# Summing a selective scan over its states chunk by chunk instead of half chunk by half chunk, in a Mamba plus mixture-of-experts block

## The chip, the cores and the metric

The kernel runs on one core of a Trainium2 chip. The metric is the device time of one execution in microseconds (us), as a median over executions. A core has five instruction queues that matter here: PE (the matrix engine; PEld are its weight loads), DVE (vector), ACT (scalar functions), POOL (a second vector engine) and SP (which only issues DMAs). Each queue runs its instructions in the order in which they were written and stops at the first one whose inputs are not ready.

## What is computed

The input is x of shape 4 x 512 x 256 in float32. First a Mamba layer with its norms and its residual, then a mixture of experts with the same:

```
proj = LN(x) @ in_proj.T;  xs, gate = split(proj)              # 512 channels each
xt   = silu(causal depthwise conv of 4 taps(xs) + conv_b)
ts, B, C = split(xt @ x_proj.T)                                # 16, 16, 16
dt   = softplus(ts @ dt_proj.T + b)
state[d,s] = state[d,s] * exp(dt[d] * A[d,s]) + dt[d] * B[s] * xt[d]     # over the time t
y[d] = sum over s of state[d,s] * C[s]                         # 16 states
x    = x + LN((y + xt * D) * silu(gate) @ out_proj.T)
out  = x + LN(shared expert / 5 + 4/5 * top-4 of 16 experts(LN(x)))
```

## The kernel before

**Tiling.** The 2048 tokens are cut into 8 units n of 256 tokens (two units are one sequence). The 512 channels are cut into 4 chunks c of 128. A chunk's states are laid on the partitions as 32 channels x 4 states, so a chunk needs 4 state groups g times 2 pairs p, which makes 8 slots; a unit has 32 slots and the kernel 256. In a slot k, ACT writes exp(dt A) into a PSUM tile `h` (L493, two instructions of 128x256), DVE runs the recurrence over 128x512 in place (`scan`, L777), and DVE multiplies with C into `hc` (`times_c`, L785), of which a ring of 11 buffers exists. POOL makes dt B x for two slots at a time (`dbx`, L505). `rep` (dt and dt x repeated over the partitions) and `bt`, `ct` (B and C likewise) come back through DRAM.

**The sum over the states.** `sum_y` (L791) adds the 4 states on neighbouring partitions, and the 4 state groups, by matmuls with the constant `sel` (128x32): each takes 32 output columns of the array and writes 32 partitions of the PSUM tile `y`, of which there is one bank. It is called for YS = 4 slots at a time, so twice per chunk and 64 times in all. One call is 8 matmuls; a float32 matmul stands in the profile as two instructions, so a call is 16 of them. When a chunk's second call is done, `close` (L811, DVE) adds D xt, `gated_y` (L817, POOL) multiplies with the gate, and `out_proj` (L887, PE) projects two chunks at a time. A chain of small steps (norm, add, norm, transpose, router, top 4) follows, and then the 10 pairs of experts of that unit: `h1`, `h3` (L1041, PE), tanh and a copy (ACT), `gated` (L1060, DVE), `weighted` and `product` (L1056 and L1063, POOL), `down` (L1072, PE). Ahead of the scans a unit needs its `front`: norm, `in_proj` (L391), `conv` (L406, PE), `x_proj` (L434), `dt_proj` (L457), softplus, and stores.

**The head.** `first()` (L509) writes unit 0's front by hand. Its end is: `x_proj`, with four spare matmuls between its halves (`warm`, L310: a 128x128 product whose result nobody reads); `ssm` on ACT; `dt_proj`; `softplus` on ACT (L463); then four groups of matmuls with `rsel` (L560) which repeat dt and dt x over the partitions for chunk 0; their copies on DVE (L563); the first exps and the first dbx. 

**Who sets the order.** Everything else is a task of the class `Plan`. A task has an engine, a duration booked by hand, a due rank (mostly its slot number), what it depends on and which ring buffers it takes. `Plan.order` (L179) plays the tasks forward with those durations and picks, on the engine that could start soonest, the task of the lowest rank among those that could start within a patience. The tables SHIFTS and PATIENCE move ranks and patience per kind of task and unit. The result is one fixed order per engine. In it, the loop at the end of the kernel fills gaps that the plan leaves on PE before the first `down` with spare matmuls, one for each 0.22 us.

Of the kernel before, what the change touches and what calls it, by code (L numbers as in the profile page):

```python
# [24 lines left out]
CI = DI // P  # L25
# [10 lines left out]
CP = CG // NJ  # L36
CSL = SG * CP
SLOTS = CI * CSL
YS = 2 * CP
FR = 42  # L40
START = 16
CH = HS // H
# [12 lines left out]


SHIFTS = dict(
    fA=(0, -12.75, 3, -15.25, 45, 15.25, 6.5, -4),
    fB=(-1.25, -13, -10, 37.25, 25.25, 41.5, 0, -11.5),
    fC=(-54, -5.25, 6, -12.75, -37.75, 17.5, -35, 24.75),  # L60
    fD=(-12, 19.5, -4, -8.5, -1.25, 44.5, -41.5, -33.5),
    exps=(14.5, 48.75, 33.5, 0, -49, 5.25, -9, 0),
    dbx=(15.25, -9.75, 10, 6, 4.75, 40.75, -9.5, 15.75),
    scan=(54.75, 16.75, -3.75, 59, 8.5, -7.75, -20, -1.5),
    hc=(37.75, -41.25, 48.5, -15.75, 3.75, 52.25, 5.75, -8.5),
    keep=(57, 0, 0.25, 0, 0, 0, 18.75, 0),
    sum=(-5, -7, 28, 41, -11.5, 11.25, 25.5, -3.5),
    close=(2.5, 19.5, 17, 12.25, 10.25, -33.5, -53, 24.5),
    ld=(0, -0.75, -11.75, 1.5, -8, -21.5, 0.75, 1.5),
    bc=(0.25, 0, 11, -13.25, 0.75, -5.75, -49, 2.75),  # L70
    chain=(-5.25, -30.5, -52, -53, -33, -45, -0.25, 6),
    load=(-20.25, -23.5, -56.75, -22.25, 2, -38.25, 0, -5.5),
    h1=(51.75, 9.5, -2.75, 11.25, 24, 23.5, 7.5, 28.75),
    h3=(28.5, -0.25, -56.5, -51.25, 2.5, 3, 4.25, 10.75),
    act=(7, 44.5, -2.25, 0, -10.25, 28.5, 10.75, 0),
    gated=(-8, -9, -29.25, -2.25, -60, -54.75, -31, -10),
    prod=(36.5, 3, -6, 5, -41, -46.25, 15.75, 23.5),
    down=(-8.5, 40.5, -32, 9.5, -10.25, 14, -8, 29.5),
    fin=(11.75, 1.25, -15, 8.5, -5.75, 29, 2.25, -6.5),
)  # L80

PATIENCE = dict(
    fA=(1.5, 1, 0.3, 0.1, 0.6, 0.6, 0.3, 0.6),
    fB=(1, 0.1, 0.1, 0.1, 0.6, 0.1, 0.1, 0.1),
    fC=(1, 0.1, 0.6, 1, 0.6, 0.1, 0.1, 0.1),
    fD=(0.6, 0.3, 0.1, 0.1, 0.1, 0.3, 0.1, 0.6),
    exps=(0.1, 0.3, 0.1, 0.1, 0.6, 0.1, 0.1, 0.1),
    dbx=(2.2, 0.3, 0.1, 0.1, 0.3, 1.5, 0.6, 0.1),
    scan=(0.1, 0.1, 0.1, 0.1, 2.2, 0.3, 0.1, 0.6),
    hc=(0.1, 0.1, 0.6, 0.3, 1.5, 2.2, 0.1, 0.1),  # L90
    keep=(0.1, 0.1, 0.1, 0.1, 0.3, 0.1, 2.2, 0.1),
    sum=(0.3, 0.6, 0.3, 0.6, 0.1, 0.3, 0.6, 0.1),
    close=(0.1, 0.1, 1.5, 0.1, 0.3, 0.3, 0.6, 1.5),
    ld=(1, 0.3, 0.1, 1.5, 0.1, 0.1, 0.1, 0.1),
    bc=(0.3, 1, 1.5, 0.6, 1, 2.2, 0.1, 0.1),
    chain=(0.6, 0.1, 0.1, 0.1, 0.1, 0.1, 0.1, 0.6),
    load=(0.6, 1, 0.3, 2.2, 1.5, 2.2, 1.5, 0.6),
    h1=(0.1, 0.3, 0.1, 0.3, 1.5, 1, 0.1, 2.2),
    h3=(0.1, 0.6, 0.1, 0.3, 1, 0.1, 0.3, 0.3),
    act=(0.6, 0.1, 0.3, 0.6, 0.3, 1, 0.1, 2.2),  # L100
    gated=(0.3, 0.6, 0.1, 0.3, 0.1, 0.3, 0.1, 1.5),
    prod=(0.6, 0.1, 0.3, 0.1, 0.1, 0.1, 0.6, 1),
    down=(0.1, 2.2, 0.1, 1.5, 0.1, 0.1, 0.1, 2.2),
    fin=(0.1, 0.1, 0.3, 0.1, 0.3, 0.1, 0.6, 2.2),
)

GROUPS = dict(
# [6 lines left out]
    scan=(SLOTS, "scan"),  # L114
    hc=(SLOTS, "hc"),
    keep=(SLOTS, "keep"),
    sum=(SLOTS // YS, "sum"),
    close=(CI, "close yg"),
    ld=(CI, "reps loadxg decay0 decay1 delta"),
    bc=(1, "bc"),  # L120
# [127 lines left out]
def mamba_then_moe(ctx: ExitStack, tc: tile.TileContext, a: dict, out: bass.AP):  # L248
# [61 lines left out]
    def warm(n, bank):  # L310
        t = ps.tile([P, P], F32, name=bank)
        for _ in range(n):
            T.matmul(t, ident, ident, start=True, stop=True)  # L313
# [111 lines left out]
                ALU.add, ALU.mult,  # L425
            )

    def x_proj(n, bank, between=lambda: None):

        t = q["x", n] = ps.tile([P, U // 2], F32, name=bank)  # L430
        q["ssm", n] = ring(work, [P, U // 2], "ssm")
        for c in range(CI):
            for h in range(2):
                T.matmul(  # L434
                    t[ts(h, P // 2), :], w_x[:, c, :], q["xt", n, c // 2][:, c % 2, ts(h, U // 2)],
                    start=c == 0, stop=c == CI - 1,
                )
            if c == 1:
                between()

    def ssm(n):
        S.activation(q["ssm", n], q["x", n], AF.Identity, bias=one_row)
# [66 lines left out]
    def first():  # L509
        st = stats_of(xs[0])  # L510
        rstd = stat.tile([P, NU], F32, name="rstd")
        G.tensor_scalar(rstd, st[:, :, 2], 1.0 / D, EPS, ALU.mult, ALU.add)
        G.tensor_tensor(rstd, rstd, mhalf, ALU.pow)
        xn = ring(work, [P, NU, D], "xn")
        for i in range(NU):
            V.tensor_scalar(
                xn[:, i, :], xs[0][:, i, :], st[:, i, 1:2], rstd[:, i : i + 1],
                ALU.subtract, ALU.mult,
            )
        xn_t = q["xn_t", 0] = ring(work, [P, CD, U], "xn_t")  # L520
        for k, nm in enumerate(("f", "h1")):
            t = ps.tile([P, U], F32, name=nm)
            for i in range(NU):
                T.transpose(t[:, ts(i, P)], xn[:, i, ts(k, P)], ident)
            (V.tensor_copy if k else S.copy)(xn_t[:, k, :], t)
        make_taps()
        for m in range(2):
            in_proj(0, m, ("h3", "y")[m])
        for m in range(2):
            xp = q["pad", 0, m] = ring(work, [P, 2, KC - 1 + U], "xp")  # L530
            G.memset(xp[:, :, 0 : KC - 1], 0.0)
            copy = V.tensor_copy if m else S.copy
# [12 lines left out]
        store_bc(0)  # L545
        rp = reps[0] = ring(work, [P, CG, 2, U], "rep")
        us = [ring(work, [P, 2, U], "u") for m in range(2)]
        dt_proj(0, ("po", "h1"))
        softplus(0)
        dt = [q["sp", 0][:, ts(m, 2), :] for m in range(2)]  # L550
        load_bc(0)
        G.tensor_tensor(us[0][:, 0, :], dt[0][:, 0, :], q["xt", 0, 0][:, 0, :], ALU.mult)

        banks = iter("f h3 y po".split())
        spread = {}
        for h in range(2):
            for w, src in enumerate((dt[0][:, 0, :], us[0][:, 0, :])):
                t = spread[h, w] = ps.tile([P, 2, U], F32, name=next(banks))
                for j in range(2):
                    T.matmul(t[:, j, :], rsel[:, 2 * h + j, :], src, start=True, stop=True)  # L560
        for h in range(2):
            for w in range(2):
                V.tensor_copy(rp[:, ts(h, 2), w, :], spread[h, w])  # L563
        for i in range(2):
            exps(i)
        inputs_of(0, 2)
        G.tensor_tensor(us[0][:, 1, :], dt[0][:, 1, :], q["xt", 0, 0][:, 1, :], ALU.mult)
        for w, t in enumerate((dt, us)):
# [250 lines left out]
    for k in range(N * SLOTS):  # L819
# [32 lines left out]
        if n % UB == 0:  # L852
            add(("keep", k), "ACT", 0.06, k - 1, lambda k=k: keep(k),
                [("scan", k)] + ([("delta", i - CI)] if n else []), (), [("h", k)])
        if k % YS == YS - 1:
            s = k // YS
            fresh = k % CSL == YS - 1
            last = c == CI - 1 and not fresh
            add(("sum", s), "PE", 1.0, k - 3 if last else k + 2, lambda k=k: sum_y(k - YS + 1),
                [("hc", k)] + ([("sum", s - 1)] if s else []),  # L860
                [("y", ("y", i))] if fresh else [], [("hc", j) for j in range(k - YS + 1, k + 1)] + [("y", i)])
            if not fresh:
                add(("close", i), "DVE", 0.385, k - 3 if last else k + 3, lambda n=n, c=c: close(n, c),
                    [("sum", s), ("loadxg", i)], (), [("y", i), ("xgt", i)])
                add(("yg", i), "POOL", 0.685, k - 3 if last else k + 3, lambda n=n, c=c: gated_y(n, c),
# [5 lines left out]
    def chain(n):  # L871
# [115 lines left out]
        def store_cw():  # L987
# [270 lines left out]
```

## Time and profile before

| | |
|---|---|
| median of 3 runs (lowest, highest) | 701.21 us (701.19, 704.19) |
| the profiled execution: its own time, its span | 703.04 us, 701.2 us |
| mean granted clock of the matrix engine | 0.993 of full speed |
| scan L777 | 256 instructions, 1220 ns each |
| hc L785 | 256 instructions, 680 ns each |
| dbx L505 | 129 instructions, 2346 ns each |
| expert matmuls L1041 and L1072 | 1280 and 640 instructions, 296.4 and 152.5 us busy |
| sum matmuls L799 | 1024 instructions, 385 ns each, 68.7 us busy |
| spare matmuls L313 | 212 instructions, 28.5 us busy |

The span runs from the first to the last instruction of the execution; the execution's own time has 1.84 us more around it. Busy time is the union of an engine's instructions, so matmuls that overlap on the array are counted once: 1024 of 385 ns make 68.7 us. The chain of waits goes back from the last instruction, at each step to what released it. The windows view gives each engine's busy time in a stretch, the number of its instructions in brackets, and the clock that was granted to the matrix engine.

### The profile page before, as it was taken

The numbers are of one execution on the slowest core, as the hardware profiler recorded it, in microseconds if no ns is written. First come the engines' busy times: TensorE is split into PE (matmuls) and PEld (weight loads), VectorE is DVE, ScalarE is ACT, GpSimd is POOL, SyncE is SP. The second block draws the span as 40 slices with busy tenths as digits, with TensorE's granted clock in tenths as the row PEclk, the third lists the DMA queues.
The fourth block names the chain that finished last, engine by engine and source line by source line (L and its number), as shares of the span: only waits on it lengthen the run. The fifth ranks groups of instructions, "written<-read, shape, count | busy, mean of one in ns | idle before, by whom it ended". The sixth has DMA issues, their size and how long they took to land.

```text
span 701.2 us, 13359 instructions
## 1 busy us (share of the span) xinstructions
PE 678.9 (97%) x4468; PEld 540.3 (77%) x4468; DVE 575.2 (82%) x814; ACT 492.9 (70%) x1308; POOL 603.6 (86%) x607
## 2 busy tenths in 40 slices
PE   8899998999999998999999999999999999999996
PEld 7777676767777776888777787778877787888885
DVE  3598999899999998998999979979899879942111
ACT  2599979889777868686888876877787767723220
POOL 1498569999999999999999999999999999975644
PEclk9999999999999999999999999999999999999999
DMA  5298766586847886669668687779687754563650
GB/s 165 101 323 275 241 209 211 161 287 220 300 164 223 278 267 208 202 241 306 235 201 269 220 263 232 243 232 318 208 254 243 243 193 151 181 212 127 218 209 18
DMA packets 84697, 155.16 MB, mean 221 GB/s; under 512 B 9842, under 2 KB 33266, under 8 KB 84628
## 3 DMA queue, kind: packets, MB, share of 16 engines
q1 hardware_dynamic: 83796, 152.99, 65.9%
q10 hardware_dynamic: 832, 1.31, 0.5%
q8 instruction: 35, 0.57, 0.3%
q14 instruction: 34, 0.28, 0.1%
HBM read 135.27 MB, written 19.01 MB: 220 GB/s over the span
## 4 chain that ended last, share of the span: by engine, by line
PE 59%; DVE 15%; ACT 11%; POOL 11%; issue 3%; POOLq 0%; DVEq 0%; ACTq 0%
PE h L1041 29%; PE po L1072 14%; DVE h L777 8%; ACT h L493 5%; PE y L799 5%; DVE hc L785 4%; POOL dbx L505 4%; PE f L894 3%; POOL g L1063 2%; PE f L391 2%; POOL g L1056 2%; PE f L406 1%; PE f L313 1%; ACT xn L355 1%; DVE q L1060 1%
## 5 line engine op out<-in xcount | busy, mean ns | idle before, releaser
L777 DVE TENSOR_TENSOR_SCAN h<-h,dbx 128x512 f32<-128x512 f32 x256 | 308.2, 1220 | 21.4 <-POOL dbx L507 8.8
L505 POOL TENSOR_TENSOR dbx<-rep,bt 128x1024 f32<-128x1024 f32 (+1 forms) x129 | 302.1, 2346 | 21.2 <-DVE h L777 16.4
L1041 PE MATMUL h<-xn_t,w 128*128 128x256 f32 x1280 | 296.4, 383 | 1.3 <-ACT g L1053 1.0
L493 ACT ACTIVATE h<-rep,a_rep 128x256 f32<-128x256 f32 x512 | 244.8, 478 | 57.2 <-DVE hc L785 43.9
L1041 PEld LDWEIGHTS h<-xn_t,w 128*128 128x128 f32 x1280 | 240.9, 191 | 43.5 <-issue 4.4
L785 DVE TENSOR_TENSOR hc<-h,ct 128x512 f32<-128x512 f32 x256 | 170.3, 680 | 3.9 <-ACT carry L789 1.8
L1072 PE MATMUL po<-w,g 128*128 128x256 f32 x640 | 152.5, 383 | 0.9 <-POOL g L1063 0.9
L1072 PEld LDWEIGHTS po<-w,g 128*128 128x128 f32 x640 | 119.1, 190 | 24.7 <-issue 4.5
L1063 POOL TENSOR_TENSOR g<-g,q 128x512 f32<-128x512 f32 x80 | 101.7, 1272 | 10.5 <-DVE q L1060 7.7
L1060 DVE SCALAR_TENSOR_TENSOR q<-th,h 128x512 f32<-128x512 f32 x80 | 54.5, 681 | 55.6 <-PE h L1041 54.4
L1056 POOL TENSOR_TENSOR g<-g,cwb 128x512 f32<-128x512 f32 x64 | 81.6, 1274 | 16.9 <-ACT g L1053 16.5
L1048 ACT ACTIVATE th<-h 128x512 f32<-128x512 f32 x80 | 47.6, 595 | 57.8 <-PE h L1041 57.5
L799 PE MATMUL y<-hc,sel 128*32 128x256 f32 x1024 | 68.7, 385 | 0.1
L799 PEld LDWEIGHTS y<-hc,sel 128*32 128x32 f32 x1024 | 27.4, 109 | 29.8 <-issue 14.7
L496 ACT COPY h<-zero 128x1 f32<-128x1 f32 x256 | 41.7, 163 | 8.2
L391 PE MATMUL f<-xn_t,w_in 128*128 128x256 f32 x176 | 42.6, 385 | 1.5 <-DVE gate L739 1.2
L391 PEld LDWEIGHTS f<-xn_t,w_in 128*128 128x128 f32 x176 | 32.6, 190 | 9.2 <-DVE gate L739 1.3
L1053 ACT COPY g<-h 128x512 f32<-128x512 f32 x64 | 37.2, 581 | 0.0
L789 ACT COPY carry<-h 128x2 f32<-128x2 f32 x128 | 19.3, 159 | 22.8 <-DVE h L777 14.7
L406 PE MATMUL h<-xp,taps 64*64 64x256 f32 x288 | 29.5, 381 | 0.6 <-DVE xt L423 0.6
L894 PE MATMUL f<-w_out,yg 128*128 128x256 f32 x112 | 26.6, 382 | 0.0
L406 PE MATMUL f<-xp,taps 64*64 64x256 f32 x208 | 25.3, 382 | 0.9 <-POOL delta L771 0.6
(163 smaller groups left out, 607.5 us busy)
## 6 DMA issues: line engine op xcount, KB each, us to landing
w<-in_w SPq DMA_DIRECT2D x80, 512.0 KB, 5.1
rep<-rep SPq DMA_DIRECT2D x124, 256.0 KB, 4.3
w<-in_w SPq DMA_DIRECT2D x80, 256.0 KB, 4.4
cwb<-cwd SPq DMA_DIRECT2D x64, 256.0 KB, 4.8
xg<-xg SPq DMA_DIRECT2D x32, 256.0 KB, 4.6
bt<-bc SPq DMA_DIRECT2D x8, 512.0 KB, 6.2
ct<-bc SPq DMA_DIRECT2D x8, 512.0 KB, 6.9
xg<-gate SPq DMA_DIRECT2D x16, 256.0 KB, 5.8
```

What stands on the lines that cost most here:

```text
L391: T.matmul(t[:, j, :], w_in[:, k, ts(2 * m + j, P)], q["xn_t", n][:, k, :], start=k == 0, stop=k == CD - 1,)
L406: T.matmul(t[j][half[r ^ j], :], taps[half[r], 2 * m + j, k, :], q["pad", n, m][half[r], j, k : k + U], start=k == 0, stop=k == KC - 1,)
L493: S.activation(h[:, j, :], dt[:, m, 0, :], AF.Exp, scale=a_rep[:, c, g, m : m + 1])
L505: G.tensor_tensor(t[:, m], reps[n * CI + c][:, m, 1, :], bt[:, m], ALU.mult)
L777: V.tensor_tensor_scan(flat, flat, dbx[:, ts(p, NJ), :].rearrange("p j t -> p (j t)"), 0.0, ALU.mult, ALU.add)
L785: V.tensor_tensor(hc, expo[k], ct, ALU.mult)
L799: T.matmul(ys[n, c][m * CS : (m + 1) * CS, :], sel, hcs[k][:, j, :], start=g == 0, stop=g == SG - 1,)
L1041: T.matmul(t[:, j, :], weights[i][:, j, ts(CD * w + k, P)], x[:, k, :], start=k == 0, stop=k == CD - 1,)
L1056: G.tensor_tensor(gs[i], gs[i], cws[i], ALU.mult)
L1060: V.scalar_tensor_tensor(t, hid[i, "th"], 1.0, hid[i, 1], ALU.add, ALU.mult)
L1063: G.tensor_tensor(gs[i], gs[i], hid[i, "q"], ALU.mult)
L1072: T.matmul(acc[n][:, t, :], gs[i][:, j, ts(t, P)], weights2[i][:, j, :], start=m == 0 and j == 0 and t == 0, stop=m == NB - 1 and j == EB - 1,
```

## The change

`sum_y` takes a list of slots. For chunks 0 to 2 it is called once, for all 8 slots; for chunk 3, the last of a unit, twice, for 4 slots each. That makes 5 calls per unit and 40 in all instead of 64. The plan books 0.125 us per slot for it, so 1.0 us for a whole chunk and 0.5 us for a half, where it booked 1.0 us for 4 slots before. In the head, two spare matmuls are added after `x_proj`'s second half and four after `dt_proj`. SHIFTS and PATIENCE are replaced as a whole. The rings, the number of instructions of DVE, ACT, POOL and SP, and all other code stay.

```diff
-YS = 2 * CP
+YS = CI + 1
...
-    sum=(SLOTS // YS, "sum"),
+    sum=(YS, "sum"),
...
-            if c == 1:
-                between()
+            if c % 2:
+                between(c)
...
-        x_proj(0, "y", lambda: warm(4, "f"))
+        x_proj(0, "y", lambda c: warm(5 - c, "f"))
...
         dt_proj(0, ("po", "h1"))
+        warm(4, "f")
         softplus(0)
...
-    def sum_y(k0):
-
-        for k in range(k0, k0 + YS):
+    def sum_y(ks):
+
+        for k in ks:
...
-        if k % YS == YS - 1:
-            s = k // YS
-            fresh = k % CSL == YS - 1
-            last = c == CI - 1 and not fresh
-            add(("sum", s), "PE", 1.0, k - 3 if last else k + 2, lambda k=k: sum_y(k - YS + 1),
+        half = c == CI - 1 and k % CSL == CSL // 2 - 1
+        final = k % CSL == CSL - 1
+        if half or final:
+            s = n * YS + c + (c == CI - 1 and final)
+            ks = range(k // CSL * CSL, k + 1)
+            if c == CI - 1:
+                ks = range(k - CSL // 2 + 1, k + 1)
+            fresh = ks[0] % CSL == 0
+            last = c == CI - 1 and final
+            add(("sum", s), "PE", 0.125 * len(ks), k - 3 if last else k + 2, lambda ks=ks: sum_y(ks),
                 [("hc", k)] + ([("sum", s - 1)] if s else []),
-                [("y", ("y", i))] if fresh else [], [("hc", j) for j in range(k - YS + 1, k + 1)] + [("y", i)])
-            if not fresh:
+                [("y", ("y", i))] if fresh else [], [("hc", j) for j in ks] + [("y", i)])
+            if final:
...
-        step("out0", "PE", 1.73, lambda: out_proj(0), [("yg", n * CI + 1)] + ([("sum", 8 * n + 6)] if n else []),
+        step("out0", "PE", 1.73, lambda: out_proj(0), [("yg", n * CI + 1)] + ([("sum", YS * n + YS - 2)] if n else []),
```

Of the tables, two rows as a sample:

```diff
-    sum=(-5, -7, 28, 41, -11.5, 11.25, 25.5, -3.5),
+    sum=(-4.75, -1, -0.5, -7.75, -13.5, -33.75, -6, 3),
...
-    down=(-8.5, 40.5, -32, 9.5, -10.25, 14, -8, 29.5),
+    down=(-0.25, 31.5, 2.5, -2, 50.25, 60, 5, 40.5),
```

More of the change, by code (lines that the diff above doesn't have):

```diff
@@ L57 @@
 SHIFTS = dict(
[L58 to L66, printed above, removed]
@@ L67 @@
-    sum=(-5, -7, 28, 41, -11.5, 11.25, 25.5, -3.5),
[L68 to L75, printed above, removed]
@@ L76 @@
-    gated=(-8, -9, -29.25, -2.25, -60, -54.75, -31, -10),
-    prod=(36.5, 3, -6, 5, -41, -46.25, 15.75, 23.5),
-    down=(-8.5, 40.5, -32, 9.5, -10.25, 14, -8, 29.5),
-    fin=(11.75, 1.25, -15, 8.5, -5.75, 29, 2.25, -6.5),
+    fA=(-8, -4, 22.75, 8.75, 23.25, -6.75, 46, -19.25),
+    fB=(0, 12.5, -42.75, 6.5, 0.5, 5.75, -7.5, 8.25),
+    fC=(16, 10, 7.25, 4.75, -5.75, -21, 0.25, -13.5),
+    fD=(-5.75, 3.5, 16.5, -0.25, -9, 59.5, -49.75, 6.5),
+    exps=(-60, -2.5, 35, -30.5, 5.75, 39.75, 3.25, 0.5),
@@ new lines @@
+    dbx=(33.25, -15, 4.25, 0, -10, -47.5, 27.5, 6.25),
+    scan=(16, 21.25, 60, 15.75, -8, 7, 28, 60),
+    hc=(16.75, 8.25, 33.25, 1.5, -23.25, 27.75, 1.5, 8.75),
+    keep=(7.75, 0, 4.75, 0, 45.75, 0, -0.5, 0),
+    sum=(-4.75, -1, -0.5, -7.75, -13.5, -33.75, -6, 3),
+    close=(3.25, 11.25, -9, -39.25, -38, -0.75, -2, 7.25),
+    ld=(4, 12.75, -29.5, -4.25, 1.25, -5.25, 8.75, 3),
+    bc=(7.5, 0, 3.75, -25.5, -15.75, -0.25, 1, 23.25),
+    chain=(-33.75, -10.75, -52, -17, -47.75, -14.5, 7.25, 0),
@@ L80 @@
+    load=(0, -43.75, -4, -36, 6.75, -1, 0.5, 18),
+    h1=(24, 20.5, 18, -18.75, 50, 9, 5.25, 10.5),
+    h3=(-49.5, 14.25, -12.5, 51.25, -37.75, 53.5, -3.5, 38),
+    act=(31.25, -10, -11, 0.75, -4.75, -3, 22.25, -2.25),
+    gated=(-5.25, 16, -7.25, -12.75, 0.75, 34, -10.5, 3),
+    prod=(15.5, -10.25, 2.75, 0.25, -28.5, 2.25, 2.25, -1.75),
+    down=(-0.25, 31.5, 2.5, -2, 50.25, 60, 5, 40.5),
+    fin=(8.75, 4.75, 1, -48.25, 3.75, 20.25, -4.25, 0),
 )
 PATIENCE = dict(
-    fA=(1.5, 1, 0.3, 0.1, 0.6, 0.6, 0.3, 0.6),
@@ L84 @@
[L84 to L104, printed above, removed]
+    fA=(1.5, 0.1, 0.1, 0.3, 0.1, 0.1, 0.3, 1),
@@ new lines @@
+    fB=(0.1, 0.1, 0.1, 0.1, 0.1, 0.6, 0.1, 0.1),
+    fC=(0.3, 1.5, 0.3, 0.6, 0.3, 0.1, 0.6, 0.1),
+    fD=(0.1, 0.6, 0.3, 2.2, 0.1, 2.2, 0.3, 2.2),
+    exps=(0.1, 0.1, 1.5, 0.1, 1.5, 0.1, 0.1, 0.6),
+    dbx=(0.3, 0.1, 0.1, 0.1, 0.1, 0.1, 0.3, 0.1),
+    scan=(0.1, 0.1, 1, 0.6, 0.1, 0.6, 2.2, 0.1),
+    hc=(2.2, 1, 0.1, 0.1, 0.6, 0.3, 0.6, 0.1),
+    keep=(0.1, 0.1, 0.3, 0.1, 1, 0.1, 0.1, 0.1),
+    sum=(0.1, 1, 0.1, 0.1, 0.6, 0.1, 1.5, 2.2),
+    close=(0.1, 0.6, 1, 0.1, 0.1, 0.6, 0.1, 0.1),
@@ new lines @@
+    ld=(0.3, 2.2, 0.1, 0.1, 1.5, 0.6, 0.1, 1),
+    bc=(1.5, 0.3, 1, 1.5, 2.2, 0.1, 2.2, 0.1),
+    chain=(0.1, 0.6, 0.3, 0.3, 0.1, 0.6, 0.1, 0.6),
+    load=(1.5, 0.3, 0.3, 0.6, 0.3, 1.5, 1.5, 1.5),
+    h1=(2.2, 0.6, 0.6, 0.1, 0.3, 0.3, 0.1, 0.1),
+    h3=(1.5, 0.6, 1, 0.6, 0.6, 2.2, 2.2, 1),
+    act=(0.1, 0.1, 0.1, 1, 0.3, 0.6, 1.5, 1),
+    gated=(0.3, 0.6, 0.1, 0.3, 0.1, 0.1, 0.3, 0.1),
+    prod=(0.1, 0.1, 0.3, 0.1, 0.1, 0.1, 2.2, 1.5),
+    down=(0.3, 1, 0.1, 0.1, 0.1, 0.6, 0.3, 0.1),
+    fin=(0.6, 2.2, 0.1, 0.6, 1.5, 0.1, 0.1, 0.1),
@@ L426, in silu, with x_proj @@
             )
-    def x_proj(n, bank, between=lambda: None):
+    def x_proj(n, bank, between=lambda c: None):
         t = q["x", n] = ps.tile([P, U // 2], F32, name=bank)
```

## The prediction

> **What bounds the kernel now.** I read the page's busy shares first, then the windows by stage, then the chain of waits. The shares and the chain's sum by engine:
>
> ```profile
> PE 678.9 (97%) x4468; PEld 540.3 (77%) x4468; DVE 575.2 (82%) x814; ACT 492.9 (70%) x1308; POOL 603.6 (86%) x607
> PE 59%; DVE 15%; ACT 11%; POOL 11%; issue 3%; POOLq 0%; DVEq 0%; ACTq 0%
> ```
>
> PE is the bound, but a share over the whole span hides the stages. The windows view (stretch, length, then busy time of PE, PEld, DVE, ACT, POOL, each with its count, and the clock) has three of them:
>
> ```profile
> 25.00:122.00 97.00, 89.68 (x783) 69.48 (x782) 90.80 (x119) 82.90 (x229) 76.58 (x83) 0.99 0.71 238
> 122.00:300.00 178.00, 174.16 (x1157) 135.16 (x1157) 167.55 (x236) 141.31 (x376) 170.54 (x164) 0.99 0.71 232
> 300.00:622.00 322.00, 321.00 (x2020) 254.72 (x2018) 294.35 (x403) 240.93 (x653) 312.10 (x302) 1.00 0.71 236
> 622.00:695.00 73.00, 72.61 (x342) 63.61 (x342) 12.93 (x28) 17.86 (x35) 39.58 (x44) 1.00 0.45 152
> ```
>
> Until 122 us DVE's scans of unit 0 set the pace, and PE's busy time there is partly spare passes. From 122.65, the first expert matmul in the timeline, to 694.7 PE is the bound, with POOL just behind it (482.6 us of the 500 up to 622). After 622 there are only experts left, and PE works alone. So a microsecond that PE saves after 122 counts in full if PE finds other work, and one in the head counts if it lies on the way to the first expert.
>
> **The sums.** The chain of waits in the PE stage shows what one costs (start, length, what); the timeline shows the one chunk in mid-kernel whose two sums happen to stand together:
>
> ```profile
> 526.87 1.73 PE po L1072 x8
> 528.59 1.00 PE y L799 x16
> 529.59 3.65 PE h L1041 x16
> ```
>
> ```profile
> 328.09 1.93 PE L799 MATMUL y<-hc,sel 128*32 128x256 f32 x32
> 329.95 1.99 PE L894 MATMUL f<-w_out,yg 128*128 128x256 f32 x8
> 331.78 1.89 PE L1072 MATMUL po<-w,g 128*128 128x256 f32 x8
> ```
>
> A lone sum takes 1.00 us, and the two groups of expert matmuls behind it 3.65 where two take 3.45 elsewhere in the chain: of that 0.20 I put half on entering and half on leaving the narrow form. Two sums in a row take 329.95 - 328.09 = 1.86. A merge therefore saves 2 x 1.00 - 1.86 = 0.14, and 0.19 more if both sums stood between full-width matmuls. How often that is so, the orders of the two programs tell. After the first expert matmul both have 54 half chunks left to sum. Before, they stand in 51 runs, and the runs of narrow matmuls (sums, conv, x_proj and dt_proj, as far as they touch) are 57; after, 34 and 44. Saved: 17 x 0.11 (a run's end) + 13 x 0.19 = 1.9 + 2.5 = **4.3 us**. The merges ahead of the first expert matmul save nothing, since DVE sets the pace there.
>
> **The spare passes in the head.** The clock of PE went to half just where the head is serial:
>
> ```profile
> 19.31:22.72 3.41, 1.84 (x22) 1.46 (x19) 0.00 (x0) 2.14 (x6) 0.42 (x1) 1.00 0.04 10
> 22.72:26.14 3.42, 3.42 (x10) 2.71 (x9) 1.14 (x2) 1.92 (x4) 0.31 (x1) 0.50 0.68 273
> 275.30:278.72 3.42, 1.62 (x20) 1.04 (x12) 3.39 (x5) 3.29 (x9) 3.34 (x6) 1.00 0.27 102
> 278.72:282.14 3.42, 3.17 (x8) 2.54 (x9) 3.21 (x13) 2.60 (x9) 3.34 (x4) 0.50 0.80 265
> ```
>
> I cut the stretches where the clock changed. Both half-speed ones last 3.42 us and follow a stretch of that length in which PE was busy 1.84 or 1.62 us, with no gap over 1.3 us (dt_proj ends at 21.2, the rsel matmuls L560 start at 22.28). Those 16 take 22.28 to 27.52, so 5.24 us, against 16/8 x 1.73 = 3.46: 1.8 us lost. The new passes (17 of them take 4.06 us at 59.8 in the timeline, so 0.24 each) fill the 0.47 us before dt_proj, in which PE waits for ACT's `ssm`, and 0.96 of the 1.1 behind it; the last ends at 21.2 + 0.96 = 22.16, before softplus does at 22.22, so they delay nothing. With 3.2 us busy of 3.4 the clock should hold. What is late next: POOL's first dbx, which began at 26.46 when the second copy was done, also needs bt, issued at 21.81; bt's landings take 3.8 at least, so it is there between 25.6 and 26.46. POOL's two half dbx (1.27 each) could end at 28.1 to 29.0 instead of 29.76, a gain of 0.8 to 1.6; I take 1.2 us.
>
> The Trainium skill ("TensorE: Matmul & The Clock Gate", the section on why this matters for your kernels) speaks against this gain: it asks only that no gap exceed about 3 us, and no gap here does. By it the passes are worth nothing and the sum would be 4.3 us. The rows above show half speed after gaps of 1.1 us.
>
> **The new order.** Ahead of the first expert matmul, PE does the same real work in both programs: four in_proj matmuls fewer (4 x 0.43 = 1.7), one conv more (1.9). DVE has four conv halves less and two gates more before the last `close` of unit 0 (-1.5 + 1.2), one hc less (-0.6). ACT still switches its function table 17 times, and the DMAs that SP issues are the same in number. So I cost the order at 0. Its bounds: from 122.65 to 694.7 are 572.0 us, and PE's groups there, each at its undisturbed length, sum to 561.5 (160 and 80 expert groups at 1.73, 13 in_proj, 14 out_proj, 54 sums at 0.89, and the rest); so 10.5 us are idle or stretched. A perfect order saves them, one twice as loose adds them. Plan and rows disagree in one thing: the plan books 1.0 us for a whole chunk's sum that takes 1.86. Spare passes placed by the plan up to the first `down` rise from 82 to 109 (5.9 us), about what the sums are booked too short by ahead of it (4 x 0.86 + 2 x 0.5 = 4.4). At worst each delays real work behind it, +4.4 us; as DVE is late anyway there, I take 0. Later the short booking does no harm that I can see: PE is then behind the plan, and what it needs is there earlier than planned.
>
> **The hc ring.** A whole chunk holds 8 of 11 buffers until its sum is done, so DVE's fourth hc of the next chunk waits for it (before: the eighth). Behind that hc stand the scans, behind these ACT's exps and POOL's dbx. Matching the 256 hc and 64 sums in order, the fourth hc after a sum's last begins 8.0 us (median) after that one's end, and the sum begins 2.1 us after it: 1.86 for the sum still leaves about 4. I cost it at 0 and keep it as a rival.
>
> **The sum.** 703.04 - 4.3 - 1.2 = 697.5 for an execution like the profiled one. The median, 701.21, lies 1.8 below that one, so the forecast is 701.2 - 5.5 = **695.7 us**.
>
> **Rivals.**
>
> *POOL takes over (same).* From 122 to 622 POOL has 17.4 us free, PE almost nothing. If POOL cannot follow, PE's 4.3 us turn into waits for `product` and only the head's 1.2 remain: 700.0 us; the spare passes' 4.4 us in the head would end there too (700.1). For it: the chain runs through POOL between 376 and 415. Against it: 73 us of experts lie after 622, where POOL is busy for 39.6, and the new order moves a pair of them forward (67 us of PE work behind the last sum, before 72).
>
> *The ring stalls DVE (slower).* In 13 of the 64 sums before, the sum began over 8.0 - 1.86 = 6.1 us after its last hc; there the three spare buffers would have stopped DVE, for 44 us in all. Half of the sums are chunk ends: 22 us, half of which may fall on time in which DVE waits anyway (38 us free from 122 to 622). That is +11 - 5.5: 706.7 us. It decides as soon as the stalls exceed the 17.4 us that POOL has free, since dbx waits for the scans.
>
> *The passes do not hold the clock.* 701.2 - 4.3 = 696.9; not told apart by the time alone, but by the clock.
>
> **Chances.** Half a percent, 3.5 us, is about what a measurement can tell from no change. The forecast, with or without the clock and with a somewhat better or worse order, has 0.66 (faster); the POOL case and its like 0.20 (same); the ring 0.14 (slower). The range takes in half of the 10.5 us that a better order could find below the forecast (690.5) and, above, the same case and a first part of the ring's (702.5).
>
> **What would show it.** Right: one or no half-speed stretch before 30 us and L560 in about 3.5 us; 40 groups of sums, whole ones at 1.86; the first expert matmul near 121.5; PE's idle time from there to the last matmul no larger. Wrong: DVE idle before hc L785 waiting for PE's sums; POOL g or dbx as what PE waits for; the first expert matmul later than 123.

## The result and the profile after

| | before | after |
|---|---|---|
| median (lowest to highest, runs) | 701.32 us (701.19 to 704.19, 4) | 713.56 us (712.05 to 714.44, 4) |
| profiled execution, its span | 703.04, 701.2 us | 713.14, 711.2 us |
| first expert matmul, last matmul | 122.65, 694.67 us | 124.17, 704.30 us |
| last hc begins | 619.2 us | 633.6 us |
| PE at half speed before 690 us | 6.8 us | 6.8 us |

The ratio is 1.0162, 95% interval 1.0131 to 1.0194. The change makes the kernel slower by 12 us (11.4 by the ratio, 10.1 between the two profiled executions); 695.7 us was forecast, with a range of 690.5 to 702.5.

The page of after, its busy shares and the chain's sum by engine:

```profile
PE 683.9 (96%) x4534; PEld 548.9 (77%) x4534; DVE 577.1 (81%) x814; ACT 492.7 (69%) x1308; POOL 603.7 (85%) x607
PE 64%; POOL 10%; ACT 9%; DVE 8%; DMA 4%; issue 3%; SPq 1%; POOLq 0%; DVEq 0%; ACTq 0%
```

Read alone, these lines tell little: PE is busy for 5 us more, the others as before within 2 us, and the span is 10 us longer. The windows show where, in the same columns as before:

```profile
25.00:122.00 97.00, 92.32 (x825) 72.62 (x823) 91.53 (x120) 82.60 (x228) 75.86 (x82) 0.98 0.69 229
122.00:300.00 178.00, 170.50 (x1140) 133.38 (x1140) 161.64 (x229) 139.54 (x373) 166.66 (x165) 1.00 0.72 233
300.00:622.00 322.00, 315.94 (x1983) 253.36 (x1982) 290.93 (x395) 236.25 (x642) 307.02 (x290) 0.99 0.72 232
622.00:695.00 73.00, 73.00 (x367) 62.66 (x366) 22.45 (x39) 23.64 (x50) 45.63 (x54) 1.00 0.54 180
```

From 122 to 622 PE, DVE and POOL each do about 9 us less in the same 500 us (486.43, 452.57 and 473.68 busy, against 495.16, 461.90 and 482.64). No engine takes over as the bound; all three became idle for the same time. After 622 DVE still has 39 instructions to do where it had 28.

The sums themselves are what the prediction said. The chain of after (start, length, what), at one of them:

```profile
191.97 1.73 PE f L391 x8
193.69 1.86 PE y L800 x32
```

There are 40 groups, and a whole one takes 1.86 us. What is new stands in the waits (who waits for whom, us in total, times, longest; the first of these lines was 43.9 us in 57 places before):

```profile
ACT h L493 <- DVE hc L786: 51.9, 58, 2.5
...
DVE xg L812 <- PE y L800: 21.2, 20, 4.6
...
POOL yg L818 <- DVE xg L812: 6.6, 8, 2.0
```

Before, DVE's `close` waited for a sum 4.7 us in 5 places; now 21.2 us in 20. Behind `close` stand DVE's next hc and scans. DVE does not wait for a free hc buffer anywhere: the ring is no part of it.

In the head, one stretch holds three things at once (chain of after; then the windows view of the same place; then DVE's rows in the timeline, where the bracket is the idle time before a row and who ended it):

```profile
65.42 3.52 PE y L800 x32
68.94 2.65 PE po L313 x22
71.59 0.44 PE f L655 x4
72.03 1.89 PE h L406 x32
```

```profile
65.50:68.91 3.41, 3.41 (x33) 1.36 (x26) 1.58 (x2) 3.38 (x4) 3.31 (x2) 0.51 0.06 17
```

```profile
65.86 1.22 DVE L778 TENSOR_TENSOR_SCAN h<-h,dbx 128x512 f32<-128x512 f32 x1
68.98 0.48 DVE L812 SCALAR_TENSOR_TENSOR xg<-xg,chan,y 128x256 f32<-128x256 f32 x1 [1.90 <-PE y L800]
```

The new passes drove the half-speed stretch out of the head's start (none before 30 us; the `rsel` matmuls L561 take 3.53 us instead of 5.24), but after has one at 65.50 that before had not. There it nearly doubles the length of a whole sum (3.52 us), and `close` waits 1.90 us for it. Then 22 spare passes, 2.65 us, stand on the chain ahead of `conv`, and 3.54 us more of them at 73.91. In the chain of before no spare pass appears between 30 and 124 us; in that of after they are 11.8% of it.

### The profile page after: what moved, and what is told of

It reads as the page before. It is cut to its first block, busy times and chain, and to the rows that moved or that the text cites. A ratio compares the mean times of both kernels' runs of the same rounds, so it can differ in the third digit from the quotient of the medians.

```text
span 711.2 us, 13457 instructions
## 1 busy us (share of the span) xinstructions
PE 683.9 (96%) x4534; PEld 548.9 (77%) x4534; DVE 577.1 (81%) x814; ACT 492.7 (69%) x1308; POOL 603.7 (85%) x607
## 4 chain that ended last, share of the span: by engine, by line
PE 64%; POOL 10%; ACT 9%; DVE 8%; DMA 4%; issue 3%; SPq 1%; POOLq 0%; DVEq 0%; ACTq 0%
PE h L1047 27%; PE po L1078 15%; PE y L800 6%; POOL dbx L505 5%; DVE h L778 4%; ACT h L493 4%; PE f L391 4%; DVE hc L786 2%; PE f L900 2%; PE f L406 2%; DMA rep<-rep 2%; PE po L313 2%; POOL g L1069 1%; PE h L391 1%; PE f L313 1%
## 5 line engine op out<-in xcount | busy, mean ns | idle before, releaser
L800 PE MATMUL y<-hc,sel 128*32 128x256 f32 x1024 | 66.4, 390 | 1.1 <-DVE hc L786 1.1
L800 PEld LDWEIGHTS y<-hc,sel 128*32 128x32 f32 x1024 | 29.9, 111 | 30.1 <-issue 12.9
L790 ACT COPY carry<-h 128x2 f32<-128x2 f32 x128 | 19.7, 160 | 21.2 <-DVE hc L786 16.2
L812 DVE SCALAR_TENSOR_TENSOR xg<-xg,chan,y 128x256 f32<-128x256 f32 x32 | 15.2, 476 | 21.2 <-PE y L800 21.2
L818 POOL TENSOR_TENSOR yg<-xg 128x256 f32<-128x256 f32 x32 | 23.3, 729 | 6.6 <-DVE xg L812 6.6
```

Source lines behind the costliest of these rows:

```text
L800: T.matmul(ys[n, c][m * CS : (m + 1) * CS, :], sel, hcs[k][:, j, :], start=g == 0, stop=g == SG - 1,)
```

## The experiments

Eighteen kernels, in the order of the questions. Ratios are to the kernel before on the same chip, with 95% intervals. "PE busy" is the page's total.

| run | what it is | median us | ratio |
|---|---|---|---|
| e1_passes | before + the six spare passes | 701.89 | 0.9981 [0.9968, 0.9993] |
| e2_merged_old_order | before's order, sums of 23 chunks whole | 712.05 | 1.0125 [1.0099, 1.0151] |
| e3_table_only | before + new tables | 752.79 | 1.0706 [1.0671, 1.0740] |
| e6_old_table | after with the old tables | 732.79 | 1.0432 [1.0405, 1.0459] |
| u1_after_split | after's order, sums in halves again | 716.21 | 1.0181 [1.0168, 1.0194] |
| e4_booked_long | after, sums booked at their length | 723.58 | 1.0296 [1.0269, 1.0324] |
| c1_booked_095 | before, sums booked 0.95 for 1.0 | 708.93 | 1.0089 [1.0069, 1.0109] |
| m1_merge_slack | e2 for 13 chunks with slack | 706.63 | 1.0058 [1.0039, 1.0077] |
| m2_merge_tight | e2 for 10 chunks without | 709.21 | 1.0089 [1.0068, 1.0110] |
| m3_merged_close_later | e2, `close` one DVE task later | 716.56 | 1.0198 [1.0172, 1.0224] |
| m4_before_close_later | before, the same | 707.35 | 1.0071 [1.0047, 1.0094] |
| k2_clock_filled | e2 + passes in three places | 709.42 | 1.0081 [1.0064, 1.0099] |
| n1_first_left_out | before, 23 half sums left out | 705.17 | 1.0028 [1.0012, 1.0044] |
| n2_second_twice | before, second half sums twice | 713.82 | 1.0168 [1.0139, 1.0197] |
| n4_first_twice | before, first half sums twice | 714.62 | 1.0162 [1.0149, 1.0175] |
| n3_groups_behind_late | before, expert matmuls twice | 735.62 | 1.0458 [1.0444, 1.0471] |
| p1_first_and_weighted_out | n1, and 27 us less on POOL | 700.08 | 0.9968 [0.9956, 0.9981] |
| p2_weighted_out | before, 27 us less on POOL | 701.34 | 0.9984 [0.9971, 0.9998] |

### Which part of the change is it?

**The passes alone.**

```diff
-        x_proj(0, "y", lambda: warm(4, "f"))
+        x_proj(0, "y", lambda c: warm(5 - c, "f"))
...
         dt_proj(0, ("po", "h1"))
+        warm(4, "f")
```

> The kernel before with only the six spare passes around dt_proj in the head. All theories agree that this part cannot be the loss: the rsel matmuls L560 should take 3.5 us instead of 5.24 and the first scans start about 1.2 us sooner. Forecast 699.5 to 701.3 us. If it is above 703, the passes disturb something and part of the loss is theirs.

0.9981, so 1.3 us (0.5 to 2.2) faster; the median of 701.89 lies above the expected range because before took 703.24 beside it. The two stretches that the prediction cut out of before, now in e1:

```profile
19.31:22.72 3.41, 3.31 (x33) 2.83 (x31) 0.00 (x0) 2.03 (x6) 0.37 (x1) 1.00 0.04 10
22.72:26.14 3.42, 3.42 (x18) 2.98 (x17) 2.13 (x4) 2.16 (x5) 0.49 (x2) 1.00 0.88 279
```

PE is busy for 3.31 us of the first, where it was 1.84, and the clock holds in the second. Every scan but the first few stands 1.2 to 1.0 us earlier to the very end. The single executions bear the mechanism out: where the mean granted clock was 0.998, e1 took 700.86 and 701.01 us and before, beside it, 700.66 to 701.18; the gain comes from the executions in which before lost its clock. The Trainium skill ("TensorE: Matmul & The Clock Gate", why this matters for your kernels) advises against idle gaps of over about 3 us and would have given these passes no value; a window of 3.41 us with gaps of 1.3 us at most was enough to lose the clock here, and the measurement decides.

**The merge alone, in the order of before.** Nothing else moves; the first call of a chunk returns and the second does all 8 slots. One more chunk is excepted: it would need a twelfth hc buffer.

```diff
-        for k in range(k0, k0 + YS):
+        i, half = divmod(k0, CSL)
+        whole = i % CI < CI - 1 and i != 24
+        if whole and not half:
+            return
+        for k in range(k0 - half if whole else k0, k0 + YS):
```

> The order of the kernel before, task for task, but the first sum of a chunk is left out where it stood and done together with the second one (23 of the 24 chunks 0 to 2; one would need a twelfth hc buffer). This is the merge without a new plan. Theory 'booking' (the plan books 1.0 us for a sum that takes 1.86, so DVE comes to close too early and stands there 21.1 us after, 4.7 before): here close stands where it stood for a sum that ended 0.86 earlier, so some of the stall must appear; PE saves about 4 us; 697 to 703. Theory 'long sums' (one long sum per chunk holds hc and delays close, whatever the order): 706 or more. Theory 'table' (the new order is loose by itself): 696 to 699, as the prediction had it.

+8.8 us. With no change of order, and with less work on PE by the prediction's own count, the merge by itself costs three quarters of the whole loss. DVE's wait for the sums is 10.7 us here, half of after's.

**The tables and the structure, crosswise.**

> The kernel before with the new rank table alone (half-chunk sums, booked 1.0 us as measured). Theory 'table': 710 us or more, PE idle from the first expert matmul on 10 us or more more than before. Theory 'booking': nothing in the table by itself costs; 698 to 706. Theory 'long sums': 698 to 706 too.

> The changed kernel with the rank table of before (sums booked at 0.125 us a slot, passes in). 'Fitted table': 725 to 760 us, so the new table is needed by the new structure and brings it down to 713.6. 'Table at fault': 700 to 710, below the changed kernel.

752.79 and 732.79. Each table is bad with the other structure. Against the new sums on the old tables the new tables are a gain of 19 us; but what they bring the new structure to is 713.56, no better than the old order with merged sums (712.05). With whole sums in both, the new order is 1.0162 - 1.0125 = 0.4% slower than the old one, and 0.6% (4 us) without the gain of the passes.

**The length of the sum within the new order.** In u1, after's order is kept and each whole sum is cut again: its first half goes to PE at the first task behind the chunk's fifth hc.

```diff
+        o = max([where["hc", i * CSL + CSL // 2]] + ([where["close", i - 1]] if i else []))
+        s = where["sum", n * YS + c]
+        o = next(j for j in range(o + 1, s + 1) if ordered[j]["eng"] == "PE")
+        if o < s:
+            extra.setdefault(o, []).append(i)
```

> The kernel after, in its own order, with the 24 whole-chunk sums cut in two again: the first half goes to PE at the first of its tasks behind the fifth hc of the chunk, so that only a half (1.00 us) stands ahead of close. Theory A (the length of the sum at the end of a chunk is what costs, in whatever order): as the merge did in the old order, +8.8 us, undone: about 713.6 - 8 = 705 to 708, and the wait of close on PE's sums falls from 21 us to below 10. Theory B (the new order costs by itself, and the long sum is nothing in an order made for it): 712 to 717, since 24 more groups stand on PE and the plan knows of none of them.

Theory A falls for this order: 716.21. The wait of `close` fell from 21.2 to 11.4 us and the time did not. So in the new order the long sum costs nothing (1.0181 against 1.0162, intervals that overlap; if anything it helps), and the order with half sums costs 1.0181 - 0.9981 = 2.0%, 14 us, beside the passes. The two parts do not add: with half sums the order costs 14 us, with whole sums 4; the merge costs 9 in the old order and -1, not told from 0, in the new one. The 14 holds for an order that was planned for whole sums and has 24 groups put in that its plan did not know of; an order planned for half sums with these tables is e3. And u1's five executions had a mean granted clock of 0.994 to 0.998, after's four 0.990 to 0.992, so at the same clock the whole sum would look somewhat better.

### Is it the booking, the wait of close?

```diff
-            add(("sum", s), "PE", 0.125 * len(ks), k - 3 if last else k + 2, lambda ks=ks: sum_y(ks),
+            add(("sum", s), "PE", 0.235 * len(ks), k - 3 if last else k + 2, lambda ks=ks: sum_y(ks),
```

> The changed kernel with its sums booked at 0.235 us a slot, so 1.88 us for a whole chunk and 0.94 for a half, as the profile shows them. Everything else, the table too, is the changed kernel's. Theory 'booking': DVE's wait at close L812 falls from 21.1 us to under 8, and the time to 704 or less. Theory 'table': 709 to 716, the wait at close may fall but not the time. Theory 'long sums': 709 to 716 with the wait still over 15 us. All with the reservation that any other booking shuffles the whole order.

None of the three theories foresaw this time. With the length booked, the wait goes (waits of e4):

```profile
DVE xg L812 <- PE y L800: 9.9, 12, 1.6
```

21.2 became 9.9 us and the kernel became 10 us slower. It is not the clock: at the same mean granted clock, 0.990, e4 took 722.63 and 722.86 us and after 713.97 and 714.44. The plan's order is another one throughout, so this does not clear the short booking; it shows that the largest new wait of the profile is no measure of the loss. The control shows how much an order alone can do: the old kernel with 0.95 booked for 1.0.

> Control for all runs in which the plan makes another order: the kernel before with its sums booked at 0.95 us instead of 1.0, nothing else. 'Fitted table' (the table was fitted to one set of durations, and any other order it yields is worse): 715 to 750 us. If the order hardly moves or is as good: 699 to 706, and the table's run with the wrong structure (752.8) says something about the table itself.

+0.9%, 6 us, for 0.05 us in a table of durations: between the two ranges.

### Is it the sums that stand right before close?

The 23 merges split in two: 13 chunks where `close` begins over 0.9 us after its sum's end in the profile of before, 10 where it follows sooner.

First those with slack (m1), then the others (m2):

```diff
-        whole = i % CI < CI - 1 and i != 24
+        whole = i in (0, 4, 6, 9, 10, 12, 14, 16, 17, 18, 28, 29, 30)
```

> The order of the kernel before, with the sums merged in 13 of the 24 chunks only: those whose close began over 0.9 us after the end of their sum before, so that a sum 0.86 us longer is still done in time. If the loss of the merge is DVE standing at close ('late close'), it is gone here and PE's 13 x 0.33 us are left: 697 to 701 us, DVE's wait at close as before (under 6 us). If merging costs in any place ('long sums' as such: the order was fitted to the shorter ones, hc held longer), about 13/23 of the 9 us of the full merge: 705 to 708.

```diff
-        whole = i % CI < CI - 1 and i != 24
+        whole = i in (1, 2, 5, 8, 13, 20, 21, 22, 25, 26)
```

> The complement: the order of the kernel before, merged in the 10 chunks whose close stood less than 0.9 us behind its sum. 'Late close': nearly the whole loss, 707 to 712, DVE's wait at close 9 us or more. 'Long sums' as such: 10/23 of it, 704 to 707.

0.58% and 0.89%: 4.1 us for 13 and 6.3 us for 10, or 0.31 us for each merge with slack and 0.63 us without. Slack halves the price and does not remove it: m1 has the time that 'long sums' gave, m2 the one of 'late close', so neither theory holds alone. The rows of m1 against those of before show how it goes at a merge with slack: where a first half is left out, at 368.9, PE's rows go from 3.2 us late to 2.2; at 373.9 the next expert matmuls wait for other engines and stand 3.0 late, so most of the lead is gone; behind the long sum at 376.8 it is 3.8. The expert matmuls in between, in before and in m1:

```profile
373.85 2.00 PE L1041 MATMUL h<-xn_t,w 128*128 128x256 f32 x8 [0.21 <-DVE xt L423]
```

```profile
376.82 1.99 PE L1045 MATMUL h<-xn_t,w 128*128 128x256 f32 x8 [0.98 <-DVE xt L423]
```

PE's idle time before them grows from 0.21 to 0.98 us. Here a lead turns into a wait, and a delay is passed on.

Moving `close` one DVE task back, so that DVE does something else while the sum runs:

```diff
+    for c in [t for t in done if t["name"][0] == "close"]:
+        at = now = done.index(c)
...
+            if done[j]["eng"] == "DVE":
+                now = j
+                break
+        done.insert(now, done.pop(at))
```

> The full merge in the old order (712.05 us), with each close put one DVE task (a scan of 1.2 us or an hc of 0.7 us) later in DVE's queue, as far as its own reader on POOL allows. 'Late close': DVE's wait at close falls from 10.7 to under 5 us and the time to 706 or less, since the scan behind close no longer waits for PE. 'Long sums': no change, 710 to 714; or worse, since the gated product and the projection behind close come later.

> Control: the kernel before with the same shift of close and nothing merged. DVE waits only 4.7 us at close there, so little can be won: 'late close' says 700 to 704, and that the shift by itself is no gain. If it is slower by 4 us or more, the chain close, gated product, projection is tight as well, and m3's time must be read against it.

The same shift costs 0.71% with half sums and 0.73% (1.0198 - 1.0125) with whole ones: it does not help the merge, though DVE's wait at `close` falls to 5.7 us, and one kind of task moved by one place costs 5 us.

### Is it the clock?

In the profile of e2, PE is at half speed for 13.7 us before 690, against 6.8. One of these stretches and the one ahead of it:

```profile
354.87:358.28 3.41, 2.10 (x21) 1.84 (x23) 3.28 (x8) 3.11 (x13) 3.41 (x4) 1.00 0.00 1
358.28:361.70 3.42, 3.42 (x33) 1.88 (x26) 3.31 (x9) 1.36 (x5) 3.32 (x5) 0.50 0.74 254
```

The half sum left out of this chunk stood in the first one, 351.8 in before; without it PE is busy for 2.10 of 3.41 us. k2 puts four spare passes in its place, here and in two other chunks:

```diff
         if whole and not half:
+            if i in (1, 13, 17):
+                warm(4, "y")
             return
```

> The kernel before's order with the sums merged in 23 chunks (712.05 us), and four spare passes (0.96 us) in the place of the first half sum that was left out of the chunks 1, 13 and 17, which stood just ahead of three of the four stretches in which PE ran at half speed. If these stretches took the time, up to 1.7 us each: three of them fewer in the trace and 707 to 709. If the clock is a side matter: 711 to 713, with or without the stretches.

In the profiled execution (707.99 us) three of the four stretches are gone and 3.4 us are left. The median is 709.42, just above the 707 to 709 of a cost by the clock; by the ratios 3.1 us of the 8.8 came back (the two intervals just touch). So the clock is about a third of what the merge costs in the old order: PE work that is saved opens a gap, and the half speed behind it can take more than the gap gave.

The time at half speed also differs between executions of one kernel, and the time with it. Of the 72 executions of before that ran beside the other kernels, those with a mean granted clock of 0.998 took 700.7 to 701.5 us, those with 0.991 or 0.992 took 703.7 to 704.7. The six of k2 go from 706.57 us at 0.997 to 711.20 at 0.991, so the passes did not keep the clock in each of them. In the two profiles after has no more half speed than before; but its four executions all had 0.990 to 0.992, and the two at 0.992 took 712.05 and 713.14 us, 7 to 9 more than before at that clock (on other chips). So 2 to 5 of the 12 us between the medians can be the clock (an estimate from these executions).

### Does PE's work set the pace at all?

n1 leaves the first half sums of 23 chunks out altogether (y lacks their states); n2 and n4 do the second, or the first, twice (those states count twice); n3 repeats four matmuls at the head of the next group of hidden matmuls behind each second sum.

```diff
+        if whole and not half:
+            return
```

> The order of the kernel before; in the 23 chunks of the full merge the first half's sum is left out and not made up for (y lacks those states), so PE has 23 x 1.2 = 27 us less to do and nothing else changes. 'PE bound' (the prediction): 674 to 680 us. 'No lead can be kept' (PE and the other engines hand over to each other so tightly that what PE gains ahead of a handover becomes a wait there): 690 to 698 us, PE's waits up by 15 us or more.

For n2; in n4 it is `not half`:

```diff
-        for k in range(k0, k0 + YS):
+        i, half = divmod(k0, CSL)
+        twice = i % CI < CI - 1 and i != 24 and half
+        for k in list(range(k0, k0 + YS)) * (2 if twice else 1):
```

> The order of the kernel before; the first half's sum stays, and the second half's is done twice (its states are added twice), so the sum ahead of close lasts 1.86 us as in the merge, and PE has 23 x 0.87 = 20 us more to do. 'PE bound': 719 to 725 us. 'No lead can be kept': also 715 to 725, since a delay at a tight handover is passed on in full. Together with the run that leaves the first halves out: if the two changes add up to the full merge's +9 us, the merge is explained as a gain that is lost and a delay that is kept.

> The kernel before, with the first half sum of 23 chunks done twice (its states count twice in y): 20 us more work on PE in the middle of each chunk, several us ahead of the second sum and close. If only delays ahead of close are passed on: 704 to 707. If a delay of PE anywhere is passed on: 711 to 714, as with the second half.

In n3, `sum_y` notes the debt and `hidden` pays it:

```diff
+        if i % CI < CI - 1 and i != 24 and half:
+            owed.append(2)
...
-        for j in range(EB):
-            for k in range(CD):
+        again = owed.pop() if owed else 0
+        for j, k in [(0, 0), (0, 1)] * again + [(j, k) for j in range(EB) for k in range(CD)]:
```

> The kernel before, with four expert matmuls (0.86 us) done twice at the head of the next group of hidden matmuls behind the second sum of 23 chunks: 20 us more work on PE as in the run with the second sum done twice, but close finds its sum on time and only the groups of matmuls behind it come late. If the delay is passed on by close and yg: near 703.9, at most 706. If it is passed on by PE's own groups: as with the doubled sums, 711 to 714.

| | PE busy, page | against before (678.9) | time, by the ratio |
|---|---|---|---|
| n1 | 661.8 | -17.1 | +2.0 us |
| n2 | 693.7 | +14.8 | +11.8 us |
| n4 | 694.5 | +15.6 | +11.4 us |
| n3 | 714.4 | +35.5 | +32.2 us |

n1's busy time holds 6.8 us more at half speed; without the 3.4 us that these lose it would be 20.5 less, 0.89 for each of the 23 sums. n3's four calls are eight instructions in the trace, so 1.73 us a time and not the 0.86 that I wrote; its 735 us answers to 40 us of work. n2 and n4 have 6.8 and 3.4 us less at half speed than before, so what was added to them is 18.2 and 17.3 us. Work added to PE thus costs 0.6 to 0.9 of its length, wherever in the chunk it stands: ahead of `close` (n2), in mid-chunk (n4) or behind (n3). So the delay does not need `close` to be passed on. (n2 lies 1 us below its ranges, n4 0.6 above the second of its own.) Work taken from PE brings nothing; 705.17 lies above both ranges that were expected. What PE saved became idle time ahead of its next inputs: from 122 to 622 us it is idle for 20.8 us, in before for 4.8. The wait that grew most is the one for `product` (PE's waits from 122 to 700 us, in before and in n1):

```profile
PE po L1072 <- POOL g L1063: 0.9, 2, 0.7
```

```profile
PE po L1076 <- POOL g L1067: 6.6, 8, 1.7
```

n1 and n2 together do to PE what the merge does, and their +2.0 and +11.8 us add up to 13.8, not to the 8.8 of e2. So the explanation of the merge as a lead that is lost and a delay that is kept is right in kind and not in size: with the second sums long, leaving the first ones out brings 3 us (1.0168 to 1.0125, intervals that overlap).

Before is near the corner: to the one side PE holds the pace, to the other something else does. The chain's sum by engine for n1 and n4:

```profile
PE 36%; ACT 20%; DVE 18%; POOL 17%; issue 5%; DMA 3%; SPq 0%; POOLq 0%; DVEq 0%; ACTq 0%
```

```profile
PE 84%; ACT 9%; DVE 4%; POOL 2%; issue 1%; POOLq 0%; DVEq 0%; ACTq 0%
```

PE's 59% in the chain of before lie between the two.

**Is POOL the something else?** p2 leaves 22 of the 64 multiplications by the routing weights out (every third block; the experts' outputs there are unweighted), p1 does so in n1.

```diff
     def weighted(i):
+        if i % 3 == 0:
+            return
```

> As the run with the first half sums of 23 chunks left out (27 us less work on PE, 705.17 us), and besides 22 of the 64 multiplications of an expert's g by its routing weights left out on POOL (every third block; 22 x 1.27 = 28 us less work there). Theory A (between 122 and 622 PE and POOL bound together, so that neither alone buys anything): with both lightened the time falls, 685 to 697. Theory B (it is the fixed order with its handovers through DVE's scans that holds the pace, whatever PE and POOL have to do): 703 to 706.

> The kernel before with only those 22 multiplications on POOL left out (28 us less work on POOL, PE's work unchanged). Theory A: PE, busy for 495 of 500 us, then holds the pace alone: 698 to 703. If POOL alone was the bound: 685 to 692. Theory B: 701 to 704.

-2.2 and -1.1 us, for 27 us less on POOL, with and without 17 us less on PE. 700.08 lies between what the two theories gave (A up to 697, B from 703), and 701.34 fits both. With both engines lightened, 2 us of 17 or more arrive, and against n1 alone 4. The window from 122 to 622 in before and in p1, and p1's chain by engine:

```profile
122.00:622.00 500.00, 495.16 (x3175) 389.88 (x3174) 461.90 (x638) 382.24 (x1028) 482.64 (x465) 1.00 0.71 234
```

```profile
122.00:622.00 500.00, 482.93 (x2894) 388.54 (x2895) 463.25 (x639) 382.75 (x1030) 465.52 (x455) 0.99 0.71 236
```

```profile
PE 42%; DVE 21%; ACT 20%; POOL 11%; issue 7%; DMA 0%; POOLq 0%; DVEq 0%; ACTq 0%
```

In p1, PE is idle for 17 of 500 us, POOL for 34, DVE for 37, ACT for 117, and DVE does the same work (638 and 639 instructions). The chain goes round all of them. What is left to set the pace is the fixed order, which these runs keep: each engine's queue stops at its next instruction, whose input is still on another engine, and what that one saves shows up as idle time one handover later. That is a conclusion from what is left: no run lightens DVE or ACT, so that the way through the scans and the exps sets the pace in p1 is not excluded. The half-speed stretches take a part back (13.7 us in n1 and p1, against 6.8: at most 3.4 us of work).

## Why the prediction was wrong, step by step

**What failed first is the sentence that carried the sum**: PE was taken for the bound because it is busy for 495 of 500 us, so that "a microsecond that PE saves after 122 counts in full if PE finds other work". n1 saves 17 us of PE's time and gains none. A full bar says that no work can be *added*; that is what n2 to n4 show, at 0.6 to 0.9 us per us. It does not say that less work would end sooner. The hint was on the page: a chain of waits with only 59% on PE is no engine's own chain. The Trainium skill ("Perfetto Trace Analysis", identifying the most-contended engine) says that the busy time of matmuls is no good measure of how near PE is to its limit and names the busy share of its weight loads as one of two better ones. Here that row stood at 390 of 500 us. n1 and p1 fit that; n2 to n4, where added work cost most of its length, do not. Its other advice, to work on the engine of the highest occupancy first, finds no support here, since lightening the two busiest brought 2 us.

**The term of the sums (4.3 us).** Its parts were right in size: 1.86 for a whole sum, 40 groups. (It prices a merge at 0.14 us by its rows and then adds it up with 0.11; with 0.14 the term would be 4.9.) As time it was worth nothing in the old order, and what it left out decides there: a merge moves 0.86 us from mid-chunk to the end. Most of the gain in the middle became waits and half-speed stretches, the delay at the end was kept in good part: e2, +8.8. In the new order u1 gives the merge -1.3 us, not told from 0.

**The new order, costed at 0 with bounds of 10.5 us either way.** This term is wrong as well: the order costs 4 us with whole sums (after against e2, the passes taken off) and 14 with half sums put into it (u1), the one inside the bounds, the other outside. The count of instructions by engine, which the zero rested on, says nothing about an order. From the first expert matmul to the last PE was idle for 4.8 of 572.0 us in before; in after it is 13.5 of 580.1, where the prediction had named "no larger" as the sign of being right. c1 and m4 give the scale: 0.05 us in one booking, or `close` moved by one place, cost 6 and 5 us. *Which* of the new order's handovers cost this was not taken apart; with orders that are made as a whole by one plan, no single one could be undone.

**"Later the short booking does no harm that I can see."** `close` waits for sums 16 us more, in 15 places more; but e4 and u1 halve that wait and are no faster. It is visible, and not shown to cost anything.

**The head.** Passes: right, 1.3 us against 1.2, and by the mechanism named; that the size agrees so well is partly luck, since it depends on how often before loses its clock there. The first expert matmul was expected near 121.5: e1 has it at 121.42, after at 124.17 (later than 123 was a sign of being wrong), so the order lost 2.75 us there. Two things are on its chain: spare passes ahead of `conv`, which the prediction had priced at 0 ("At worst each delays real work behind it"), and half speed at 65.5, which it did not have. No run parts them from the rest of the order; e4, which books the sums long, still has 123.57.

**The rivals.** *POOL takes over* was right that PE's saving turns into waits, and gave 700 for it; that POOL alone is the bound is refuted by p2, and p1 leaves little of POOL and PE together (2 us, with at most 3.4 more lost to half speed). *The ring* had the sign and nothing else: DVE waits for no buffer. *The passes do not hold the clock* fell with e1. None of the rivals was that a new order costs by itself.

Of the kernels that compute the whole result e1 alone is faster than before, by 1.3 us.

## What to carry to other kernels

An engine that is busy for 99% of a stretch is only shown to be full; test whether it is the bound by leaving some of its work out, and by adding some, before pricing a saving on it. Where several engines run one fixed, interleaved order, shortening a step in the middle can be lost at the next handover while lengthening one is mostly passed on; so price a merge by what it delays, not by what it saves. And a new order is a cost of its own with a range taken from what small moves of the order do (5 and 6 us here), never a zero because the counts agree.

## What the runs showed of the hardware

PE's clock went to half for stretches of 3.41 us, or twice that. The three shown here followed stretches of the same length in which PE was busy for 1.62 to 2.10 us, with gaps not over 1.3 us. With six spare passes there (e1: busy for 3.31 us), or four (k2), the clock held in the profiled execution. The busy share alone does not decide it: in after PE is busy for 1.62 us from 229.30 to 232.71, and the next 3.42 us run at full speed. With PE work left out the profiles show more half speed before 690 us, with work added less: 13.7 us in n1, e2 and p1, 6.8 in before, 3.4 in n3 and n4, none in n2. It is not only the work: m4 and c1, which change the order alone, and m2, with ten merges, have 3.4. And it differs from one execution to the next: the mean granted clock was 0.987 to 0.989 in n1's seven, 0.991 to 0.998 in before's, 0.994 to 0.999 in those of n3 and n4.
